# Layers 1 to 3 of a graph network: node phases cut into pieces, messages in steps, TensorE in source order

## The chip, the cores and the metric

The kernel runs on one core of a Trainium2 chip. The metric is the device time of one execution in microseconds (us), median over runs; lower is better. The engines are named as the profile names them: PE is TensorE (PEld its weight loads), DVE is VectorE, ACT is ScalarE, POOL is GpSimd, SP is SyncE, whose queue only issues DMAs.

## The reference

A graph of 12500 nodes with 64 features and 212500 edges (sorted by destination, self-loops among them) goes through four layers; each is wrapped as `x = layernorm(x + layer(x))`:

```
L0  attention, 4 heads:  h = x@W; e = leaky(a_src[src] + a_dst[dst]); softmax over each node's edges; sum of h[src]*alpha
L1  three times:         h = x@Ws[i]; x = relu(segment_sum(norm * h[src], dst) + bs[i]);   then x@W_out + b_out
L2  five times:          h = leaky(x@W1+b1)@W2 + b2;  e = leaky(edge_attr@We1+be1)@We2 + be2
                         x = layernorm(x + segment_sum(h[src]*e*dot_scale, dst)*res_w)*g + b
L3  once:                h = elu((segment_sum(x[src], dst)/count) @ W); batchnorm(h)*gamma + beta
```

Layers 0 and 1 add one more self-loop to every node. There are nine passes over the edges after layer 0: three in layer 1, five in layer 2, one in layer 3.

## The kernel before

The nodes lie in 128 blocks of 98 (`NQ`, `QB`); four blocks are a group (`G`), so 32 groups. A preparation sorts each destination block's edges into 16 columns of 128 slots (`NJ`). Fourteen of them (`NG`) hold rows that a one-hot matmul of the source block makes: `gather_block` (L924) multiplies a source block's table by one-hots `oh` (fp8) for all 128 destination blocks at once, 14 times 3 matmuls of 98x64 (L931), copies the result from PSUM to `hb` on ACT (L932) and writes it to the DRAM table `g_d` (L933, L934). The last two columns are fetched by two indirect gathers on POOL from the plain node table `tq_d` (`fetch`, L1496).

A pass, `run_pass`, walks the 128 destination blocks. `ask(d)` requests a block's data: the destination one-hots `hot` (L1504), in layer 2 the transposed edge attributes `et` (L1808), the rows `hg` from `g_d` (L1494), and the two gathers. It runs `AHEAD` = 4 blocks ahead. In layers 1 and 3 the row itself is the message; in layer 2 `edge_message` makes it: two matmuls of 128x512 (L1783; the profile shows two records for each f32 matmul), bias and leaky relu on ACT and DVE (L1438, L1439), the second dense layer into two PSUM banks (L1792, L1797), a product with `hg` (L1802). `add_up_parts` cuts the f32 message into three bf16 parts that are read in place: `top` is the upper half of each f32, two subtractions (L1520) leave the remainders, and 16 matmuls with `hot` (L1522) sum the 128 slots by destination, all three parts at once. After two blocks `sums` (L1536) adds the three parts from PSUM into `xsum`.

After the fourth block of a group `node(g, ...)` runs the whole node phase: layer 1 `conv_out` (which adds the node's own row `told`) and `conv`, in its third pass `last_conv` (two dense layers, a layernorm and the first layer 2 node network), layer 2 `node2` (layernorm L1414 to L1429, then `node_network`: transposes L1390, L1696, leaky, L1398), layer 3 `node3`. It ends in `spread`: `split3` (L919 to L922) turns the new table into three bf16 parts by turns on ACT and DVE, the table goes to `tq_d`, and four `gather_block` calls follow one another. The one-hots `oh` for them are loaded at the group's start, in `states(g)` (`load_ohs`, L1511).

While layers 0 and 1 run, `pump` issues indirect gathers of edge attributes on POOL (L959), two and one a block by turns in layer 1; `settle` transposes the arrived ones on PE (L948), ACT copies (L950) and writes them to `at_d` for layer 2. A transposition waits for one gathered tile more before it is put into the program.

The order of work: POOL and SP run in the order of the source (`tc.manual_schedule(engines={POOL, SP})`). PE, DVE and ACT are ordered by the framework's scheduler, which places instructions by its own estimate of their times. Every engine executes its list in order. Each PSUM tile is a bank; layer 2 uses all eight (`pgat` 2, `pacc` 1, `pnode` 1, `p1` 2, `pe` 2).

Of the kernel before, what the change touches and what calls it, by code (L numbers as in the profile page):

```python
# [865 lines left out]
def tile_gnn_resnorm_d4(ctx: ExitStack, tc: tile.TileContext, a: dict, out: bass.AP):  # L866
# [70 lines left out]
    room = {}  # L937
# [3 lines left out]
    def settle(keep):  # L941

        while len(late) > keep:
            d, lo, n, ag = late.pop(0)
            pt = room["ps"].tile([P, QA // 4, P], F32, name="pattr", bufs=1)
            for q in range(n // 4):
                tc.keep_in_program_order(
                    pe.transpose(pt[:, q, :], ag[:, 4 * q:4 * q + 4, :].rearrange("p u f -> p (u f)"), ident))  # L948
            ab = room["sb"].tile([P, QA // 4, P], F32, name="ab", bufs=room.get("ab", 1))
            tc.keep_in_program_order(sca.copy(ab[:, :n // 4, :], pt[:, :n // 4, :]))  # L950
# [371 lines left out]
    def network():  # L1322
        with ExitStack() as s0:
# [178 lines left out]
            def load_hot(d):  # L1502
                hot = wk.tile([P, NJ, P], F8, name="hot", bufs=AHEAD + 3)
# [11 lines left out]
            def add_up_parts(hot, x, ps):  # L1515

                top = x.rearrange("p k j f -> p (k j f)").bitcast(BF16).rearrange(
                    "p (k j f h) -> p k j f h", k=3, j=NJ, h=2)[:, :, :, :, 1]
                for k in range(2):
                    v.tensor_tensor(x[:, k + 1], x[:, k], top[:, k], op=OP.subtract)  # L1520
                for j in range(NJ):
# [17 lines left out]
            def run_pass(gd, tab, message, node, states, attrs=(), extra=None):  # L1539
                k = 0  # L1540
                ready = []

                def ask(d):
                    hot = load_hot(d)
                    ex = extra(d) if extra is not None else None
                    ready.append((fetch(d, D, gd, tab, message is None), hot, ex))
# [3 lines left out]
                for g in range(NGR):  # L1550
                    st = states(g)
                    xsum = nt("xsum", DH)[:, :, :D]
                    for pr in range(2):
                        ps = ps_tile([P, 2, 256], "pacc")
                        for i in range(2):
                            d = G * g + 2 * pr + i
                            if d + AHEAD < NQ:
                                ask(d + AHEAD)
                            if attrs:
                                pump(attrs[k % len(attrs)])  # L1560
                                k += 1
                            hg, hot, ex = ready.pop(0)
                            add_up_parts(hot, hg if message is None else message(hg, ex), ps[:, i, :3 * D])
                        sums(xsum, pr, ps, D)
# [374 lines left out]
```

## Time and profile before

| | |
|---|---|
| median of 17 runs | 11363.62 us (11336.18 to 11391.89) |
| the profiled execution | 11402.6 us, span of its instructions 11400.7 us |
| PE busy | 8751.3 us, 77% (weight loads 7324.0 us) |
| DVE busy | 8622.8 us, 76% |
| POOL busy | 6576.8 us, 58% |
| ACT busy | 3871.8 us, 34% |
| DMA | 2414.80 MB, 212 GB/s on average |
| layer 0 begins its gathers | 1652 us |
| first sum of layer 1, of layer 2, of layer 3 | 3539, 5912, 10750 us |

The three passes of layer 1 take 713, 696 and 806 us from their first to their last sum, the five of layer 2 928, 928, 923, 921 and 898 us, that of layer 3 471 us; between one pass's last sum and the next one's first lie 42, 40, 76, 52, 50, 48, 47 and 46 us.

How to read it: shares of the whole span mix stages with different limits, so a table by stage is needed. An engine's busy time leaves out what lies between its instructions: between POOL's gathers the timeline always shows 0.30 us. Ends of matmuls are modelled and overlap with the next one's start; the distance from start to start tells what one costs. A wait that the profile names ("<-") is put down to what ended it.

### The profile page before, as it was taken

To read this page: it belongs to the slowest core of one execution; us is meant where nothing else is said; L and a number is where in the kernel's file an instruction comes from. 1 tells how busy PE (TensorE), PEld (TensorE's weight loads), DVE (VectorE), ACT (ScalarE), POOL (GpSimd) and SP (SyncE) were. 2 spreads that over 40 slices of the span, in tenths; PEclk is the share of its full clock that TensorE was granted. 3 is DMA by queue.
4 is the path that set the end of the run, shared out by engine and by line. 5 is a ranking of instruction groups with operands and counts; after the bars stand their busy time and mean duration, and the time that the engine had idled before them with its cause. 6 is when DMAs were issued, how large, how long until landed. Compare 5 with 4: busy or idle time off the path is not lost.

```text
span 11400.7 us, 260491 instructions
## 1 busy us (share of the span) xinstructions
PE 8751.3 (77%) x102114; PEld 7324.0 (64%) x102115; DVE 8622.8 (76%) x16365; ACT 3871.8 (34%) x7061; POOL 6576.8 (58%) x4616
## 2 busy tenths in 40 slices
PE   2332468888886666667689999999999999899762
PEld 2110458888886665666567777777777777677652
DVE  5889447888885545555568887887887888799888
ACT  2431235455552222222233333333333333333200
POOL 0667578777775767776635544553554555344482
PEclk9855668889987777877789999999999999999875
DMA  2663675555556878877777767776776877677673
GB/s 78 224 224 103 201 244 151 150 153 154 157 151 205 262 249 271 274 246 230 230 238 242 237 212 241 238 239 218 240 241 208 252 241 240 215 250 255 213 212 86
DMA packets 1377992, 2414.80 MB, mean 212 GB/s; under 512 B 421097, under 2 KB 732537, under 8 KB 1376625
## 3 DMA queue, kind: packets, MB, share of 16 engines
q1 hardware_dynamic: 734770, 1565.65, 43.4%
q10 hardware_dynamic: 494495, 714.10, 17.4%
q0 software_dynamic: 147488, 118.29, 6.8%
q8 instruction: 807, 13.22, 0.5%
q14 instruction: 432, 3.54, 0.1%
HBM read 1655.94 MB, written 741.25 MB: 210 GB/s over the span
## 4 chain that ended last, share of the span: by engine, by line
PE 39%; DVE 23%; DMA 19%; issue 8%; ACT 4%; POOL 3%; ACTq 1%; SPq 1%; POOLq 0%; DVEq 0%
PE pacc L1522 8%; PE pe L1797 7%; PE pgat L931 7%; PE p L1783 6%; DMA hg<-tq_d,q_ovr 4%; PE pacc L1532 3%; DMA hg<-g_d 3%; DVE msg L1520 3%; DMA g_d<-hb 3%; PE prank L1603 3%; DVE top L1165 2%; ACT sg L1175 2%; DMA ag<-in_edge_attr_dram,q_eid 2%; PE pnode L1398 2%; DMA slb<-sl_d 2%
## 5 line engine op out<-in xcount | busy, mean ns | idle before, releaser
L1496 POOL DMA_INDIRECT hg<-tq_d,q_ovr x2304 | 3644.4, 1582 | 3130.1 <-DVE msg L1802 1524.7
L959 POOL DMA_INDIRECT ag<-in_edge_attr_dram,q_eid x2048 | 2601.0, 1270 | 1196.5 <-issue 547.0
L931 PE MATMUL pgat<-t,oh 98*128 98x64 bf16 x48384 | 1881.2, 201 | 448.9 <-DVE t L922 195.9
L931 PEld LDWEIGHTS <-oh 98*128 98x128 fp8e4 x48384 | 1801.2, 103 | 643.8 <-issue 620.1
L1522 PEld LDWEIGHTS <-hot 128*128 128x128 fp8e4 x18432 | 1714.1, 103 | 746.1 <-issue 655.3
L932 ACT COPY hb<-pgat 128x448 f32<-128x448 f32 (+1 forms) x2560 | 1302.5, 536 | 2141.7 <-PE pgat L931 1317.8
L1520 DVE TENSOR_TENSOR hg<-hg 128x1024 f32<-128x1024 f32 x1024 | 1237.3, 1220 | 887.2 <-DMA hg<-tq_d,q_ovr 457.0
L1520 DVE TENSOR_TENSOR msg<-msg 128x1024 f32<-128x1024 f32 x1280 | 1557.9, 1217 | 3.9
L1797 PEld LDWEIGHTS pe<-we,eh 128*128 128x128 f32 x10240 | 1364.1, 192 | 225.1 <-issue 140.9
L1797 PE MATMUL pe<-we,eh 128*128 128x128 f32 x10240 | 1469.0, 279 | 4.5 <-DVE eh L1439 3.4
L1438 ACT ACTIVATE eh<-p,be 128x512 f32<-128x512 f32 x1280 | 875.7, 687 | 1567.3 <-PE p L1783 1262.5
L1522 PE MATMUL pacc<-hg,hot 128*128 128x192 bf16 x8192 | 1031.6, 285 | 415.1 <-DVE hg L1520 240.2
L1783 PE MATMUL p<-et,we 128*128 128x512 f32 x2560 | 1290.1, 606 | 22.1 <-DMA et<-at_d 14.7
L1802 DVE TENSOR_TENSOR msg<-pe,hg 128x512 f32<-128x512 f32 x1280 | 862.4, 683 | 322.3 <-PE pe L1797 266.4
L1522 PE MATMUL pacc<-msg,hot 128*128 128x192 bf16 x10240 | 1033.7, 248 | 33.0 <-DVE msg L1520 25.1
L1439 DVE SCALAR_TENSOR_TENSOR eh<-eh 128x512 f32<-128x512 f32 x1280 | 856.9, 682 | 66.2 <-ACT eh L1438 47.1
L1603 PE MATMUL prank<-rv,h 128*128 128x161 f32 x4096 | 742.0, 339 | 202.5 <-DVE rv L1601 162.5
L1603 PEld LDWEIGHTS prank<-rv,h 128*128 128x128 f32 x4096 | 674.7, 218 | 230.7 <-DVE rv L1601 188.1
L1178 PE MATMUL taken<-sg,hotc 128*128 128x456 bf16 x512 | 245.1, 556 | 551.7 <-ACT sg L1175 546.0
L1783 PEld LDWEIGHTS p<-et,we 128*128 128x128 f32 x2560 | 420.6, 192 | 248.1 <-issue 119.4
L1532 PE MATMUL pacc<-msg,o 128*128 128x68 f32 x4096 | 543.3, 295 | 30.7 <-DVE msg L1652 30.7
L1536 DVE TENSOR_REDUCE xsum<-pacc 98x128 f32<-98x384 f32 x576 | 318.0, 552 | 315.2 <-PE pacc L1522 314.1
(327 smaller groups left out, 10278.2 us busy)
## 6 DMA issues: line engine op xcount, KB each, us to landing
hg<-g_d SPq DMA_DIRECT2D x1152, 448.0 KB
g_d<-hb ACTq DMA_DIRECT2D x1152, 416.0 KB
hot<-hot_d SPq DMA_DIRECT2D x1152, 256.0 KB
oh<-oh_d SPq DMA_DIRECT2D x1152, 171.5 KB
et<-at_d SPq DMA_DIRECT2D x640, 256.0 KB
vb<-vw_d SPq DMA_DIRECT2D x128, 912.0 KB
hg<-g_d SPq DMA_DIRECT2D x128, 476.0 KB
g_d<-hb ACTq DMA_DIRECT2D x128, 442.0 KB
```

What stands on the lines that cost most here:

```text
L931: pe.matmul(ps[:, j, :], lhsT=oh[:, 7 * hf + j, :], rhs=t3(k), start=(k == 0), stop=(k == 2))
L932: sca.copy(hb[:, 7 * hf:7 * hf + 7, :], ps)
L959: pool.indirect_dma_start(out=ag[:, j, :], out_offset=None, in_=a["edge_attr_32"], in_offset=bass.IndirectOffsetOnAxis(ap=eid[:, d, lo + j ...
L1438: sca.activation(dst, ps, AF.Identity, bias=bias)
L1496: pool.indirect_dma_start(out=hg[:, NG + i, :], out_offset=None, in_=tab, in_offset=bass.IndirectOffsetOnAxis(ap=ovr[:, d, i:i + 1], axis= ...
L1520: v.tensor_tensor(x[:, k + 1], x[:, k], top[:, k], op=OP.subtract)
L1522: pe.matmul(ps.rearrange("p (k f) -> p k f", k=3), lhsT=hot[:, j, :], rhs=top[:, :, j, :], start=(j == 0), stop=(j == NJ - 1))
L1532: pe.matmul(ps, lhsT=o32[:, j, :], rhs=x[:, hf * nj + j, :], start=(hf + j == 0), stop=(hf == 1 and j == nj - 1))
L1603: pe.matmul(pk[:, i // 2, i % 2, :RANKS * H + 1], lhsT=h32[:, j, :], rhs=rv[:, j, :], start=(hf + j == 0), stop=(hf == 1 and j == nj - 1))
L1783: pe.matmul(p1.rearrange("p q e -> p (q e)"), lhsT=w["we1"][:, j].rearrange("p t d -> p (t d)"), rhs=et, start=True, stop=True)
L1797: pe.matmul(ps[:, u:u + 2, :].rearrange("p t d -> p (t d)"), lhsT=h1[j][:, (2 * hf + q) * P:(2 * hf + q + 1) * P], rhs=w["we2"].rearrange( ...
L1802: v.tensor_tensor(msg[:, half, :], ps, hg[:, half, :], op=OP.mult)
```

## The change

It does five things, all in the part after the preparation.

1. **Node phases in pieces.** The node functions become generators: each `yield` ends a piece. `run_pass` keeps a list `going` and takes one piece of each per block. A transposition, a dense layer, and each of the four `gather_block` calls is a piece of its own: eight pieces for layer 2's node phase, seven in layer 1's first two passes, ten in its third. A group's last gather is so issued up to ten blocks after its last sum. In layer 0 all pieces run at once.
2. **Messages in steps.** Step d does the hidden layer of block d (`first`), message and cut of block d-1 (`second`, `cut`), the sum of block d-2. Without messages (layers 1 and 3) the cut is of block d and the sum of d-1.
3. **PE in the order of the source** in layers 1 to 3 (`tc.manual_schedule(engines={PE})`).
4. **Table parts as upper halves.** `spread` cuts the table as `add_up_parts` cut the messages: two subtractions on DVE in an f32 tile of three parts, the upper halves read in place; no casts on ACT. Layer 0's softmax maxima (`a3`) are cut likewise.
5. **Loads and buffers.** `load_ohs` moves from `states` into `spread`; the buffers of `oh` go from 12 to 8, of `hg` from 6 to 7 (6 in layer 3), of `hot` from 7 to 8.

```
-            def run_pass(gd, tab, message, node, states, attrs=(), extra=None):
...
+            def run_pass(gd, tab, node, states, attrs=(), first=None, second=None, extra=None):
+                lag = 1 if first is None else 2
+                asked, begun, made, going = [], [], [], []
...
+                d = 0
+                while d < NQ + lag or going:
+                    if d + AHEAD < NQ:
+                        ask(d + AHEAD)
+                    if d < NQ:
+                        if attrs:
+                            pump(attrs[k % len(attrs)])
+                            k += 1
+                        full, hot, ex = asked.pop(0)
+                        begun.append((full, hot, None if first is None else first(ex)))
+                    if lag - 1 <= d < NQ + lag - 1:
+                        full, hot, h1 = begun.pop(0)
+                        if first is not None:
+                            full = second(full, h1)
+                        made.append((hot, full, cut(full)))
+                    if lag <= d < NQ + lag:
+                        c = d - lag
+                        g, i = divmod(c, G)
+                        if i == 0:
+                            st = states(g)
+                            xsum = nt("xsum", DH)[:, :, :D]
+                        if i % 2 == 0:
+                            ps = ps_tile([P, 2, 256], "pacc")
+                        hot, full, top = made.pop(0)
+                        add_up_parts(hot, top, ps[:, i % 2, :3 * D])
+                        if i % 2 == 1:
+                            sums(xsum, i // 2, ps, D)
+                    for t in list(going):
+                        if next(t, going) is going:
+                            going.remove(t)
+                    if lag <= d < NQ + lag and i == G - 1:
+                        going.append(node(g, xsum, *st))
+                    d += 1
...
-            def spread(g, t, ohs, cur, also=None):
-                t3 = nw.tile([QB, G, 3, D], BF16, name="t3")
-                split3(nw, t, lambda k: t3[:, :, k, :], [QB, G, D], "ns")
+            def spread(g, t, cur, also=None):
+                ohs = load_ohs(g)
+                top = cut(t)
+                t = t[:, 0]
                 sca.dma_start(group(tq_d[cur], g), t)
                 if also is not None:
                     sca.dma_start(group(also[0], g), also[1])
                 for i in range(G):
-                    gather_block(wk, pp, G * g + i, lambda k, i=i: t3[:, i, k, :], D, g_d[cur], ohs[i], hbbufs)
+                    yield
+                    gather_block(wk, pp, G * g + i, lambda k: top[:, k, i, :], D, g_d[cur], ohs[i], hbbufs)
...
+            def node_network(g, src, w, cur, also=None):
+                yield
+                xt = turned4(src)
+                yield
                 ph = ps_tile([P, G * QB], "pnode")
-                pe.matmul(ph, lhsT=w["w1"], rhs=turned4(src).rearrange("p b n -> p (b n)"), start=True, stop=True)
+                pe.matmul(ph, lhsT=w["w1"], rhs=xt.rearrange("p b n -> p (b n)"), start=True, stop=True)
                 h1 = nw.tile([P, G, QB], F32, name="nh1")
                 leaky(h1.rearrange("p b n -> p (b n)"), ph, w["b1"])
+                yield
                 ps = dense(h1, w["w2"])
...
-            hgbufs, ohbufs, hbbufs = AHEAD + 2, 3 * G, 4
+            hgbufs, ohbufs, hbbufs = AHEAD + 3, 2 * G, 4
             room.update(ag=4, ab=2)
+            phase.enter_context(tc.manual_schedule(engines={PE}))
```

## The prediction, made before the changed kernel was run

> **What bounds the kernel now.** I read the slices first, then one row per pass, then the instructions inside a pass.
>
> From the page:
> ```profile
> span 11400.7 us, 260491 instructions
> ...
> PE   2332468888886666667689999999999999899762
> ...
> DVE  5889447888885545555568887887887888799888
> ...
> POOL 0667578777775767776635544553554555344482
> PEclk9855668889987777877789999999999999999875
> ```
> From about 3500 us to 5900 PE is at 6 and 7, POOL at 7; from there to 10700 PE is at 9, DVE at 7 and 8. Two different limits, so I cut the span at the passes. A pass has 64 sums (L1536), one for two blocks; each row but the first runs from a pass's first sum to its last, that is 126 blocks. The rows: layer 0 whole, the three passes of layer 1, the first and the last pass of layer 2, layer 3. Columns: length, then busy time and count of PE, PEld, DVE, ACT, POOL, then granted clock, DMA share, GB/s.
> ```profile
> 1650.00:3510.00 1860.00, 1552.94 (x16063) 1495.62 (x16064) 1486.17 (x3660) 926.70 (x1375) 1399.35 (x1024) 0.88 0.50 149
> 3539.40:4252.60 713.20, 472.25 (x7436) 440.48 (x7436) 391.08 (x499) 178.72 (x401) 537.11 (x436) 0.80 0.83 261
> 4294.30:4990.30 696.00, 468.64 (x7440) 437.47 (x7440) 391.21 (x499) 178.76 (x405) 534.18 (x431) 0.81 0.86 269
> 5030.30:5835.80 805.50, 571.87 (x7697) 505.64 (x7696) 499.82 (x943) 209.40 (x478) 478.93 (x392) 0.74 0.75 237
> 5911.80:6839.40 927.60, 905.05 (x10248) 717.36 (x10247) 790.30 (x1412) 349.86 (x645) 445.41 (x240) 0.99 0.75 233
> 9807.00:10704.70 897.70, 860.38 (x9940) 681.15 (x9940) 846.12 (x1747) 318.77 (x616) 404.20 (x240) 0.99 0.75 246
> 10750.30:11221.50 471.20, 310.91 (x2388) 273.44 (x2386) 373.63 (x529) 40.62 (x94) 383.18 (x243) 0.77 0.70 203
> ```
> In layer 1 POOL is the limit, though its share does not say so: the timeline shows 0.30 us between any two gathers. Pass 1: 436 gathers of 537.1/436 = 1.23 us plus 0.30 are 5.30 us a block, and a block takes 713.2/126 = 5.66. Pass 2: 5.27 of 5.52. Pass 3: 392 x (1.22 + 0.30) = 4.73 of 6.39; here no engine is full, and 1.66 us a block is waiting. Layer 3: 243 x (1.58 + 0.30) = 3.63 of 3.74. Layer 0: 1024 x (1.37 + 0.30) = 1710 of 1860 us.
>
> In layer 2 the first four passes (927.6, 927.5, 922.6 and 920.8 us) take 7.34 us a block on average. PE's ends are modelled, so I take start to start. PE in the timeline of the fourth of these passes:
> ```profile
> 9306.19 0.22 PE L931 MATMUL pgat<-t,oh 98*128 98x64 bf16 x2 [0.56 <-ACT t L921]
> ...
> 9311.20 1.39 PE L931 MATMUL pgat<-t,oh 98*128 98x64 bf16 x42
> 9312.42 0.25 PE L1522 MATMUL pacc<-msg,hot 128*128 128x192 bf16 x1
> ...
> 9317.36 1.88 PE L1783 MATMUL p<-et,we 128*128 128x512 f32 x4
> 9319.09 1.52 PE L1522 MATMUL pacc<-msg,hot 128*128 128x192 bf16 x16
> 9320.45 1.52 PE L1797 MATMUL pe<-we,eh 128*128 128x128 f32 x12
> 9321.81 1.02 PE L1783 MATMUL p<-et,we 128*128 128x512 f32 x2
> ```
> Undisturbed, a block costs PE 1.73 (four L1783) + 1.36 (sixteen L1522) + 1.81 (sixteen L1797 at 1.36/12) + 0.44 (two L1792 at 0.22) + 1.22 (42 L931), and a group of four blocks 0.85 (L1696) + 0.67 (L1398) + 0.36 (L1390) = 1.88, so 0.47 a block: **7.03 us**. The 0.31 left are stalls like the 0.56 of the first line, where PE stands at a gather until ScalarE has cut a table part (L921). DVE needs 790.3/126 = 6.27. The last pass has no node network: PE 6.56, DVE 846.1/126 = 6.72, measured 7.12.
>
> **The change, part by part.** All terms are against the profiled execution: 11402.6 us, span 11400.7.
>
> *Layer 2, first four passes.* PE now runs in source order, which the order of the built program shows: hidden layer of block d, message of d-1, sum of d-2, then one piece of a node phase, with one block's gather (1.22 us) as the usual piece. No matmul is removed. Each is fed by work of the step before, so the 0.31 mostly goes. I keep 0.05 for DVE, which is 6.27 of 7.08 busy: 7.08 against 7.34 over 504 blocks is **-131 us**. Bounds: at the floor -156; below nothing if DVE's node bursts reach PE (second rival).
>
> *Last pass of layer 2.* DVE is next: 6.72 plus what gaps remain. I take 6.95 against 7.12: **-22** (bounds 0 and -50).
>
> *Table parts.* Before: cast, subtract, cast, subtract (L919 to L922), 0.40 and 0.42 us each, by turns on ACT and DVE. Now two subtracts on DVE; the parts are read in place as upper halves, at every second bf16. That access is not new: L1522 reads its 192 columns so, at 85 ns, and L931's 64 contiguous ones take 29; in proportion to L1522's columns they would take 28, so the stride costs nothing. Gone are two casts a group on ACT, which has time (349.9 of 927.6); they matter only where the chain is bare, between passes.
>
> *Layer 1, passes 1 and 2.* Neither a gather nor a transfer is removed. POOL keeps 5.30 and 5.27, DMA is already at 0.83 and 0.86. I take 5.45 and 5.42: **-26 and -13** (bounds: at POOL's floor -45 and -32; at worst +20 for both, see the clock below).
>
> *Layer 1, pass 3.* Its waits are the node phase's (two transposes, two dense layers, a norm in one chain) and POOL standing behind it. Cut in ten pieces, the chain runs beside the next blocks. What is late next: POOL at 4.73, but a gather that meets DVE work is slower: in the timeline between two layer 2 passes twelve of them take 1.00 us with DVE idle, and the one at 7854.71, beside a pair of L1520, 1.86. The mean is 1.22 here with DVE at 0.62, 1.58 in layer 3 with DVE at 0.79. At 5.6 us a block DVE stands at 3.97/5.6 = 0.71; between the two rows a gather is then about 1.41, and POOL needs 3.11 x 1.71 = 5.3. DMA moves the same bytes: 0.75 x 6.39/5.6 = 0.86, the share of pass 2. I take 5.6: **-100**. Bounds: -145 at 5.25, and -30 if only the lost casts count.
>
> This slowing has a rule. The Trainium skill, "SBUF — State Buffer", section "Who interferes with whom", says that a DVE instruction with two SBUF inputs holds up only a GpSimd instruction that reads SBUF, and infers that generating descriptors is not slowed by it. The rows say otherwise, or an indirect gather counts as a reader: layer 3's 1.58 stands beside two-input subtracts for the most part. By the rule's inference a gather would stay at 1.00 and pass 3 could reach 3.11 x 1.30 = 4.0 on POOL; the sum does not use it.
>
> *The loads of the one-hots* (four of 171.5 KB a group) leave the start of the group and move behind its dense step on SP, past the requests of some eight later blocks. Each request waits for a buffer of three blocks back (seven buffers of `hg` now, six before), so SP still runs two to three steps, 10 us or more, ahead of the gather that needs them. The four issues took 7.93 us at 4513 with SP blocked, 2.78 at 7857 unblocked; I put nothing, and if they come late PE stands for up to 2.8 us a group (bound: 2.8 x 256 = +717, far off, since SP would have to have lost its whole lead).
>
> *In-order waits.* The attribute transposes (L948) can now hold PE when their gather is late. Queued behind is the sum of the block before, and for that POOL's buffers wait. But the gathers of a tile are issued at least 2.7 blocks earlier on POOL, some 14 us, against 4.6 us from the last issue of `g_d` (7844.81) to the load that waits for it (7849.41): nothing, bound +0.3 us for each of layer 1's blocks, +115.
>
> *Between passes* (40 to 76 us, eight times): the chain sum, norm, node network, gathers, write, load stays bare. It loses two casts and their handovers (about 1 us); pieces of the group before now stand in it, with 448 KB of writes each; PE no longer puts the next pass's hidden layer between the last gathers: **-2 each, -16** (+2 to -4 each). *Layer 3*, on POOL: **-3** (bounds -14 and +10). *Layer 0*, on POOL, keeps its scheduled PE: **0** (bounds ±20).
>
> Sum: -131 - 22 - 26 - 13 - 100 - 16 - 3 = **-311**. The profiled execution is 39 us above the median of the 17 runs, 11363.6; off the median, 11363.6 - 311 = 11053, say **11050**.
>
> **The clock.** Layer 1 was granted 0.74 to 0.81, layer 2 0.99 and 1.00; the fourth slice shows 0.5. With PE's work spread thinner the grant may fall. At half, layer 1's blocks would cost PE about twice 2.9 = 5.8 in passes 1 and 2 and twice 3.5 = 7.0 in pass 3 (start to start as above), so PE would bind all three: (0.14 + 0.28 + 0.61) x 126 = +130 in place of -139. Against it: pass 3 of today idles longer at a stretch (its chain) and still gets 0.74.
>
> **Rivals.**
> 1. *Only the chain in layer 1 was bare.* Layer 2's stalls come back as waits for DVE. Then -100 - 39 - 16 - 3 = -158: about 11205. For it: DVE at 0.85. Against: the stalls seen wait on the table parts and node chain.
> 2. *Slower: the norm's burst on DVE.* A layer 2 step gives DVE 2 x 1.22 + 4 x 0.68 + 0.28 = 5.44 us of 7.08, 1.64 to spare; the norm and the line before it add 4.6 us in one or two steps. In source order PE cannot take other work while it stands at a sum. If the overhang of 4.6 - 1.64 = 3 us is not absorbed, each of 160 groups costs PE 3 us: +480 on the -311, about 11530. It starts once DVE trails PE by more than the 3.9 us (hidden layer 1.73, message 1.81 + 0.44) that a step puts ahead of its sum, and ends slower once a group loses more than 311/160 = 1.9 us. The order of the built program spreads the norm over two steps, which speaks against it.
> 3. *Nearly no effect:* layer 1's clock halves (+130) while layer 2 gains (-153), and -19 for the rest: about 11320.
>
> **How the numbers follow.** Forecast 0.63 (10900 to 11140), rival 1 0.20, rival 2 0.12, rival 3 0.05, of which 0.03 within 0.2% (about what a measurement of this kernel can tell from no change) and 0.01 on either side. Faster 0.63 + 0.20 + 0.01 = 0.84, same 0.03, slower 0.12 + 0.01 = 0.13. The range goes from all floors together (-156 - 50 - 77 - 145 - 14 - 32 = -474, about 10900) through rival 1 to 11290, where rival 2 at half its price ends (-311 + 240); 11320 and 11530 stay out.
>
> **What would show it.** Right: four passes near 892 us between first and last sum, PE without waits on table parts, pass 3 near 706, POOL's idle time there gone and its gathers longer. Wrong: PE waiting for `msg` (L1524 then) once a group, PE waiting for the one-hots' DMA or for `ag`, a clock near 0.5 in layer 1, or pass 3 still over 6 us a block.

## The result, and the profile after

The changed kernel takes 11869.5 us (median of 8 runs, 11839.0 to 11889.6) against 11363.6 of the kernel before: a ratio of 1.0441, 95% interval 1.0427 to 1.0454. It is slower, on the other side of the forecast. The profiled execution has a span of 11872.4 us, 472 more than before.

The page's first lines:
```profile
span 11872.4 us, 259968 instructions
...
PE   3331668888876666655579999998998999888762
...
DVE  6889348888765555544458878887887887887788
...
POOL 0666678777657777744434434443443443333382
PEclk9755678888877878766679999999999999888876
```
Two stretches have thinned out: the slices 18 to 20 (5050 to 5940 us), where PE falls to 5 and POOL from 7 to 4, and the slices 35 to 37 (10090 to 10980), where PE is at 8 in place of 9. The passes tell which they are. Rows as for the kernel before: layer 0, the three passes of layer 1, the first and the last pass of layer 2, layer 3 (length, busy time and count of PE, PEld, DVE, ACT, POOL, granted clock, DMA share, GB/s).
```profile
1650.00:3510.00 1860.00, 1576.18 (x16116) 1526.36 (x16117) 1479.29 (x3659) 911.19 (x1252) 1346.31 (x1024) 0.86 0.50 149
3538.70:4224.30 685.60, 456.81 (x7480) 431.42 (x7478) 387.79 (x499) 160.85 (x345) 529.82 (x435) 0.80 0.87 272
4259.60:4941.60 682.00, 452.86 (x7468) 427.71 (x7466) 386.28 (x499) 160.47 (x349) 521.47 (x430) 0.80 0.88 275
4982.20:6051.80 1069.60, 603.30 (x7758) 548.48 (x7756) 508.15 (x951) 196.40 (x423) 465.58 (x390) 0.69 0.58 178
6125.50:7055.80 930.30, 887.64 (x10191) 723.97 (x10190) 803.01 (x1401) 323.46 (x579) 418.28 (x238) 0.99 0.71 230
10088.50:11185.20 1096.70, 905.18 (x9850) 730.87 (x9849) 876.74 (x1744) 299.04 (x552) 381.66 (x238) 0.89 0.62 198
11230.60:11691.80 461.20, 315.43 (x2388) 267.25 (x2386) 373.51 (x528) 40.62 (x94) 373.67 (x243) 0.76 0.70 208
```
Term by term, forecast and measured:

| | forecast us | measured us | off by |
|---|---|---|---|
| layer 1, passes 1 and 2 | -26, -13 | -27, -14 | -2 |
| layer 1, pass 3 | -100 | +264 | +364 |
| layer 2, first four passes (930.3, 930.1, 930.4, 930.3) | -131 | +22 | +153 |
| layer 2, last pass | -22 | +199 | +221 |
| the eight gaps between passes | -16 | +37 | +53 |
| layer 3 | -3 | -10 | -7 |

The six terms add up to 471 of the 472 us; layer 0 (forecast 0) ended 0.7 us earlier. No engine has much more to do: in the third pass of layer 1 DVE's busy time rose by 8 us and PE's by 31, while its granted clock fell from 0.74 to 0.69; the pass rose by 264. The loss is standing. This is who stands, in each place.

**Layer 2, first four passes.** PE, between two sums of one of them:
```profile
7617.47 1.52 PE L1530 MATMUL pacc<-msg,hot 128*128 128x192 bf16 x16
7618.83 1.40 PE L931 MATMUL pgat<-tnew,oh 98*128 98x64 bf16 x42
7621.40 0.53 PE L1390 MATMUL pnode<-q_ident,x 98*64 98x98 f32 x4 [1.16 <-DVE x L1429]
```
PE stands once a group at the transposes, until DVE's last line of the norm (L1429): 170.8 us in the four passes together. The stalls at the table parts (L921 before) are gone, but they were small: in the kernel before, all of PE's waits in its four passes sum to 63.0 us, 10.2 of them at table parts.

**Layer 2, last pass.** PE, then DVE, around one group's first gather:
```profile
10715.83 1.52 PE L1530 MATMUL pacc<-msg,hot 128*128 128x192 bf16 x16
10723.02 0.21 PE L931 MATMUL pgat<-tnew,oh 98*128 98x64 bf16 x1 [5.67 <-DMA hot<-hot_d]
...
10725.95 2.61 PE L1825 MATMUL p<-et,we 128*128 128x512 f32 x4
```
```profile
10722.45 0.42 DVE L1425 TENSOR_TENSOR tnew<-y,ln_r 98x256 f32<-98x256 f32 x1
10722.91 0.89 DVE L1524 TENSOR_TENSOR tnew<-tnew 98x256 f32<-98x256 f32 x2
10729.71 0.69 DVE L1849 TENSOR_TENSOR msg<-pe,hg 128x512 f32<-128x512 f32 x1 [5.91 <-PE pe L1844]
```
The name behind PE's 5.67 is a load of `hot`, which this matmul does not read; what it reads and waits for is `tnew`, whose norm ends at 10722.87. (Of PE's 191.5 us of waits in this pass 81.0 are put down to that line of the norm, 96.5 to `hot`.) Only then can PE go on to the next hidden layer, and now DVE stands 5.91 us for the message. The two engines, each about 7 us busy a block by the row (905.2 and 876.7 over 126), take turns, and a block takes 8.7.

**Layer 1, pass 3.** PE, DVE and POOL in the same 20 us:
```profile
5501.01 1.61 PE L931 MATMUL pgat<-tnew,oh 98*128 98x64 bf16 x42
5514.31 0.86 PE L1390 MATMUL pnode<-q_ident,x 98*64 98x98 f32 x4 [11.69 <-DVE x L1425]
```
```profile
5504.93 0.41 DVE L1420 TENSOR_REDUCE ln_var<-ln_sq 98x4 f32<-98x256 f32 x1
5510.42 1.23 DVE L1524 TENSOR_TENSOR hg<-hg 128x1024 f32<-128x1024 f32 x1 [5.08 <-issue]
...
5513.83 0.43 DVE L1425 TENSOR_TENSOR x<-y,ln_r 98x256 f32<-98x256 f32 x1
```
```profile
5502.79 1.75 POOL L1496 DMA_INDIRECT hg<-tq_d,q_ovr  x1 [0.31 <-issue]
...
5518.00 0.99 POOL L1496 DMA_INDIRECT hg<-tq_d,q_ovr  x1 [10.81 <-PE pacc L1530]
```
PE waits for the norm's end. DVE is in the middle of the norm and stands before a cut. That cut needs rows whose second gather POOL began at 5502.79, since only PE's last sum, ending at 5501.2, had freed the buffer; the gather's packets ended at 5510.2 in the trace, and the cut began. POOL's next gather waits for PE's next sum. It is a ring of PE, POOL and DVE that turns once a group. DVE's instructions are placed by the scheduler, which puts the cuts as far ahead of the sums as the seven buffers allow.

I give the ring a number, the *room*: the sums ahead of a group's transposes on PE, plus the buffers, less the blocks cut ahead of the norm's last line on DVE. At 0, the last cut ahead of the norm waits for the very sum behind which PE stands. Sums and cuts are counted in blocks from the pass's start, by the order in the trace. The third group has 16 sums, 7 buffers, 23 cuts: 16 + 7 - 23 = 0, and 28 of the 32 groups have 0. The kernel before had 5 to 6.

**Gaps in layer 2.** PE, then SP's queue, at the start of the third pass:
```profile
8068.81 2.40 PE L931 MATMUL pgat<-tnew,oh 98*128 98x64 bf16 x42 [0.46 <-ACT hb L932]
8082.47 3.40 PE L1825 MATMUL p<-et,we 128*128 128x512 f32 x4 [11.26 <-DMA et<-at_d]
```
```profile
8058.33 0.60 SPq L1484 DMA_DIRECT2D we<-in_L_gnn_We_dram  x1
8075.31 0.35 SPq L1494 DMA_DIRECT2D hg<-g_d  x1
...
8076.19 0.42 SPq L1855 DMA_DIRECT2D et<-at_d  x1
```
Before, the hidden layer of the next pass ran between the last gathers. Now its attributes `et` are asked for behind the first `hg` load, since the new `ask` calls `fetch` first, and that load waits for the pass before to write `g_d`: SP issues nothing from 8058.93 to 8075.31.

### The profile page after: what moved, and what is told of

It is laid out like the page before. It is cut to its first block, busy times and chain, and to the rows that moved or that the text cites. A ratio compares the mean times of both kernels' runs of the same rounds, so it can differ in the third digit from the quotient of the medians.

```text
span 11872.4 us, 259968 instructions
## 1 busy us (share of the span) xinstructions
PE 8790.6 (74%) x102114; PEld 7482.1 (63%) x102115; DVE 8716.5 (73%) x16365; ACT 3673.4 (31%) x6423; POOL 6354.5 (54%) x4616
## 4 chain that ended last, share of the span: by engine, by line
PE 42%; DVE 28%; DMA 14%; issue 8%; ACT 3%; POOL 2%; SPq 1%; ACTq 0%; POOLq 0%; DVEq 0%
PE pgat L931 8%; PE p L1825 8%; PE pacc L1530 8%; PE pe L1844 7%; DVE msg L1524 4%; PE pacc L1540 4%; DMA hg<-tq_d,q_ovr 4%; PE prank L1636 3%; DVE msg L1849 3%; DVE hg L1524 2%; DVE top L1165 2%; DVE eh L1439 2%; DMA slb<-sl_d 2%; ACT sg L1175 2%; DMA hg<-g_d 2%
## 5 line engine op out<-in xcount | busy, mean ns | idle before, releaser
L1496 POOL DMA_INDIRECT hg<-tq_d,q_ovr x2304 | 3465.8, 1504 | 3971.0 <-DVE msg L1849 2183.3
L959 POOL DMA_INDIRECT ag<-in_edge_attr_dram,q_eid x2048 | 2562.7, 1251 | 984.4 <-issue 578.4
L932 ACT COPY hb<-pgat 128x448 f32<-128x448 f32 (+1 forms) x2560 | 1350.6, 535 | 3877.8 <-PE pgat L931 2835.4
L931 PE MATMUL pgat<-tnew,oh 98*128 98x64 bf16 x48384 | 1861.2, 200 | 724.1 <-DVE tnew L1719 321.5
L1524 DVE TENSOR_TENSOR hg<-hg 128x1024 f32<-128x1024 f32 x1024 | 1242.8, 1220 | 1146.8 <-DMA hg<-tq_d,q_ovr 592.8
L1530 PEld LDWEIGHTS <-hot 128*128 128x128 fp8e4 x18432 | 1767.1, 104 | 255.9 <-issue 163.6
L1524 DVE TENSOR_TENSOR msg<-msg 128x1024 f32<-128x1024 f32 x1280 | 1561.0, 1220 | 13.7
L1844 PE MATMUL pe<-we,eh 128*128 128x128 f32 x10240 | 1355.9, 276 | 0.0
L1530 PE MATMUL pacc<-msg,hot 128*128 128x192 bf16 x10240 | 977.7, 247 | 1.5 <-DVE msg L1524 0.9
L1825 PEld LDWEIGHTS p<-et,we 128*128 128x128 f32 x2560 | 456.5, 199 | 470.2 <-issue 336.1
L1540 PE MATMUL pacc<-msg,o 128*128 128x68 f32 x4096 | 581.8, 310 | 79.1 <-DVE msg L1684 77.6
L1540 PEld LDWEIGHTS pacc<-msg,o 128*128 128x128 f32 x4096 | 566.1, 224 | 92.3 <-DVE msg L1684 68.4
```

Of the source, the lines that this page charges most:

```text
L931: pe.matmul(ps[:, j, :], lhsT=oh[:, 7 * hf + j, :], rhs=t3(k), start=(k == 0), stop=(k == 2))
L932: sca.copy(hb[:, 7 * hf:7 * hf + 7, :], ps)
L959: pool.indirect_dma_start(out=ag[:, j, :], out_offset=None, in_=a["edge_attr_32"], in_offset=bass.IndirectOffsetOnAxis(ap=eid[:, d, lo + j ...
L1496: pool.indirect_dma_start(out=hg[:, NG + i, :], out_offset=None, in_=tab, in_offset=bass.IndirectOffsetOnAxis(ap=ovr[:, d, i:i + 1], axis= ...
L1530: pe.matmul(ps.rearrange("p (k f) -> p k f", k=3), lhsT=hot[:, j, :], rhs=top[:, :, j, :], start=(j == 0), stop=(j == NJ - 1))
L1540: pe.matmul(ps, lhsT=o32[:, j, :], rhs=x[:, hf * nj + j, :], start=(hf + j == 0), stop=(hf == 1 and j == nj - 1))
```

## The experiments

Theory 1: the norm stands too near, in the source, to the piece of PE that needs it. Theory 2: in layer 1's third pass the scheduled cuts close the ring. Theory 3: the order of the first loads makes the gaps. The main rival is that DVE or POOL is simply full, or that the table parts or the pieces cost something.

The runs came in five sets, each beside runs of the kernel before on the same chip. Two of the sets ran on chips where the kernel before takes 12442 and 12472 us, not about 11350; there layer 0, the first two passes of layer 1 and the gaps are longer in every kernel, layer 2's passes are the same, and the third pass of layer 1 is longer in some kernels and not in others. So those two sets are compared within themselves. Edits without an interval have one run each.

### One cause at a time

*An extra step behind the norm.*
```diff
 def node_network(g, src, w, cur, also=None):
     yield
+    yield
...
                         layernorm(y2, full[:, 0])
+                        yield
```


> One edit on the changed kernel: a node phase does nothing for one more step behind a layer norm (at the head of the node network, and behind the second norm of layer 2's last pass), so that DVE has a whole step more before TensorE reaches the piece that needs the norm. Theory 1 (TensorE in source order stands at the piece behind the norm, since the norm takes DVE more than one step): layer 2's first four passes go from 930 us each to 880 to 895 (the 0.34 us a block at the transposes goes), the last pass from 1097 to 870 to 920, layer 1's third pass from 1070 to 850 or less. Theory 2 (in layer 1's third pass DVE's own order, with cuts 5 to 7 blocks ahead of the sums, closes a loop through the buffers of gathered rows): layer 2 as in theory 1, but the third pass of layer 1 stays over 950, since the norm still stands behind a cut whose rows wait for TensorE. Rival (DVE is simply full, the standing is where its lack of time shows): all passes within 10 us of the changed kernel.

Measured: 11438.9 us. Rows of layer 1's third pass, then the first and the last of layer 2:
```profile
4970.10:6028.40 1058.30, 574.18 (x7715) 524.88 (x7713) 499.47 (x949) 185.00 (x421) 440.54 (x390) 0.71 0.58 179
6101.90:6980.30 878.40, 875.75 (x10148) 717.85 (x10147) 799.30 (x1401) 317.09 (x576) 369.61 (x238) 1.00 0.77 243
9872.20:10751.10 878.90, 833.68 (x9800) 686.22 (x9798) 852.43 (x1739) 294.77 (x550) 420.80 (x238) 0.99 0.77 246
```
Layer 2 is as theory 1 says: 930 to 878 and 1097 to 879, by one `yield` each. DVE does the same work in it, so it was not full. Layer 1's third pass stays at 1058, as theory 2 says: room there is still 0 (17 sums, 24 cuts).

*VectorE in source order in layer 1.*
```diff
-            phase.enter_context(tc.manual_schedule(engines={PE}))
+            phase.enter_context(tc.manual_schedule(engines={PE, DVE}))
```


> One edit on the changed kernel: in layer 1 VectorE's instructions too stand in the order of the source (there a cut stands one block ahead of its sum, not 5 to 7). Nothing changes in layers 2 and 3. Theory 2 (loop through VectorE's look-ahead): the third pass of layer 1 goes from 1070 us to 690 to 780, passes 1 and 2 stay within 15 us of 686 and 682. Theory 1 alone (the norm is too near to the transposes, wherever the cuts stand): the third pass keeps over 950 us. Rival (POOL: gathers slowed by VectorE's work bind the third pass): it stays over 1000 us, with no waits of TensorE on L1425 but on the cuts.

Measured: 11440.5 us. Layer 1's first and third pass:
```profile
3549.00:4193.50 644.50, 452.38 (x7482) 428.40 (x7481) 409.19 (x501) 156.04 (x345) 506.11 (x435) 0.82 0.92 290
4907.10:5633.30 726.20, 546.82 (x7801) 489.58 (x7800) 543.27 (x962) 195.52 (x426) 447.32 (x390) 0.81 0.84 264
```
Theory 2 holds: 1070 to 726, with room 7 (12 sums, 12 cuts). Passes 1 and 2 fell too, to 644 and 642, which no theory had said (expected: within 15 of 686 and 682).

*Each block's small loads first*, one-hots and attributes ahead of gathered rows, as before the change:
```diff
-                    asked.append((fetch(d, D, gd, tab, first is None), load_hot(d),
-                                  extra(d) if extra is not None else None))
+                    hot = load_hot(d)
+                    ex = extra(d) if extra is not None else None
+                    asked.append((fetch(d, D, gd, tab, first is None), hot, ex))
```


> One edit on the changed kernel: a block's one-hots and edge attributes are asked for ahead of its gathered rows, as in the kernel before. Theory 3 (at the start of a layer 2 pass the attributes stand on SP behind a load of gathered rows, which waits for the pass before to write them, so the hidden layers of the first blocks cannot run in the gap): the four gaps between layer 2's passes go from 60.3, 59.2, 62.5, 59.9 us to 46 to 54 each, together 30 to 55 us less; the passes themselves stay within 10 us. Rival (the gaps are longer because the pieces of the last groups and the one-hots' loads stand in the chain): gaps within 3 us of the changed kernel's.

Measured: 11854.2 us; the four gaps 54.3, 53.4, 56.6 and 54.0, 23.6 us less together. Half of theory 3's effect (expected 30 to 55, and no gap over 54): now the second block's attributes stood behind the first block's rows, 10.8 us.

*PE placed by the scheduler again*, all else as changed (the three `manual_schedule` lines taken out):

> One edit on the changed kernel: TensorE's instructions are placed by the scheduler in layers 1 to 3 again, and all else (pieces, steps, cuts, order of loads) stays. If the order of the source is what costs: layer 2's last pass falls from 1097 us to 850 to 900, layer 1's third pass from 1070 to 690 to 810, layer 2's first four from 930 to 890 to 925. If the pieces or the two subtracts that take the place of two casts on ScalarE cost it (VectorE's work, more of it and on one engine): the last pass of layer 2 stays over 1050 us and the third of layer 1 over 1000.

Measured: 11207.3 us, against 11343.8 of the kernel before on the same chip (one run each). Third pass of layer 1, first and last of layer 2:
```profile
4990.10:5743.60 753.50, 569.74 (x7509) 493.25 (x7506) 498.85 (x928) 176.95 (x409) 473.13 (x389) 0.76 0.79 247
5831.50:6724.90 893.40, 885.80 (x10191) 717.57 (x10191) 793.12 (x1400) 315.29 (x579) 405.55 (x238) 1.00 0.75 240
9647.80:10515.10 867.30, 832.19 (x9786) 677.81 (x9798) 834.87 (x1739) 292.87 (x550) 469.27 (x238) 1.00 0.75 249
```
So the rest of the change is a gain (-31 us a pass in layer 2's first four against the mean 924.7 of before), and PE's order of the source alone turned it into a loss. The gaps in layer 2 stay at 59.4 to 61.3 us: they do not come from PE's order.

### On a chip with longer layers 0 and 1 (kernel before: 12442 us)

*The first two edits, and the first loads ahead.* The last is this:
```diff
-                for d in range(AHEAD):
-                    ask(d)
+                for d, soon in enumerate([early(d) for d in range(AHEAD)]):
+                    ask(d, soon)
```
where `early(d)` loads a block's one-hots and attributes, and `ask` then only fetches.

> Three edits on the changed kernel: the extra step behind a norm, VectorE in source order in layer 1, and, at the start of every pass, the one-hots and edge attributes of the first blocks asked for ahead of all gathered rows. If the three causes are separate, their measured gains add: layer 2 as with the extra step alone (878 us a pass), layer 1 as with VectorE in order (644, 642, 726 or less), the four gaps between layer 2's passes 46 to 54 us instead of 60: a span of 10950 to 11010, 3 to 4% under the kernel before. If they share a cause, the span stays over 11100.

Measured: ratio 0.968 (0.965 to 0.971). Layer 2 at 878.5, 878.8, 878.9, 878.8 and 876.8; layer 1's passes take 739, 731 and 971 us and layer 2's gaps 66.1 to 68.1, which say nothing beside the set before.

*VectorE in source order in layers 2 and 3* (the same edit of `engines` there):

> One edit on the changed kernel: in layers 2 and 3 VectorE's instructions too stand in the order of the source (no extra step; layer 1 as in the changed kernel). It asks whether in layer 2 the norm is too near by the source alone, or by where the scheduler puts its second half on VectorE. By nearness alone: layer 2's passes keep 915 to 940 us and the last one over 1000. By VectorE's scheduled order: 880 to 905 and 870 to 930. Layer 3 has no norm in its pass and cuts 1 to 3 blocks ahead: 461 us within 10.

Measured: 911.4, 909.7, 911.6, 910.1 and 1062.7; layer 3 463.2. The last pass lies inside the band for nearness, and PE still stands 100 us there for `tnew`: the norm is too near by the source. The first four lie just under the band, but not for that reason. PE and DVE there:
```profile
9848.54 0.53 PE L1390 MATMUL pnode<-q_ident,x 98*64 98x98 f32 x4
...
9853.92 1.53 PE L1530 MATMUL pacc<-msg,hot 128*128 128x192 bf16 x16 [0.90 <-DVE xsum L1544]
```
```profile
9848.05 0.43 DVE L1429 TENSOR_TENSOR x<-y,b 98x256 f32<-98x256 f32 x1
...
9853.32 0.55 DVE L1544 TENSOR_REDUCE xsum<-pacc 98x128 f32<-98x384 f32 x1
```
With the norm in one piece PE's standing at the transposes falls from 170.8 to 15.0 us in the four passes. DVE is late by the norm instead, and PE stands 89.9 us at a sum, until `xsum` has emptied the one bank `pacc`. So there the late norm comes from where the scheduler puts its second half; without that the burst costs PE at the sum, some 20 us a pass less.

*Table parts as upper halves alone, on the kernel before*, in layers 1 to 3 (`top` is the view of the upper halves of `t`, which now has three planes):
```diff
-                t3 = nw.tile([QB, G, 3, D], BF16, name="t3")
-                split3(nw, t, lambda k: t3[:, :, k, :], [QB, G, D], "ns")
+                for k in range(2):
+                    v.tensor_tensor(t[:, k + 1], t[:, k], top[:, k], op=OP.subtract)
```


> One part of the change alone, on the kernel before: in layers 1 to 3 the table parts are upper halves (two subtracts on VectorE, read by TensorE at every second bf16) and no longer two casts and two subtracts by turns. If that access cost TensorE anything, layer 2's first four passes would grow by its share (42 matmuls a block: 10% on each is 0.12 us a block, 15 us a pass). If it costs nothing, they stay within 5 us or fall by up to 20 (the stalls at the gathers), the gaps fall by 1 to 2 us each, and the whole is 0 to 0.7% faster than before. In either case the loss of the whole change, 4.4%, is not here.

Measured: ratio 1.0049 (1.0032 to 1.0067), a little slower, not faster as expected; run again below.

*First loads ahead alone:*

> One edit on the changed kernel: at the start of every pass the one-hots and attributes of all the first blocks are asked for ahead of any gathered rows (with only each block's own order turned round, the second block's attributes still stood behind the first block's rows, 10.8 us, and the gaps fell by 6 us each). Theory 3: the four gaps between layer 2's passes go to 45 to 51 us from 60. Rival (the rest is the writes and the one-hots' loads of the last groups): they stay at 53 or more. The passes stay within 10 us.

Measured: 64.5, 63.7, 65.1 and 59.4 us, which this chip leaves open (the run with VectorE in order in layers 2 and 3, whose loads are the changed kernel's, had 72.9 to 73.8).

### The same again where the kernel before takes 11350 us, and two steps in place of one

> The kernel with the three edits once more (extra step, VectorE in order in layer 1, first loads ahead): the set before ran on a chip where the kernel before took 12442 us and layers 0 and 1 were longer for every kernel, so its layer 1 and its gaps say nothing beside the first set. Where the kernel before takes about 11350: separate causes give layer 1 passes of 640 to 650, 640 to 650 and 690 to 730, layer 2 passes of 878, gaps between them of 46 to 55 and a whole of 10930 to 11010, a ratio of 0.965 to 0.972. If the extra step and VectorE's order are one cause in layer 1, the third pass stays at 726 or more.

Measured: 11033.7 us, ratio 0.9719 (0.9703 to 0.9736); gaps 52.2 to 53.6; passes of layer 1 650, 641 and **782**: worse than with VectorE in order alone (726).

> First loads ahead alone, once more beside a kernel before of about 11350 us. Theory 3 alone: the four gaps between layer 2's passes 45 to 51 us (60 in the changed kernel, 54 with only each block's order turned round). Rival (the rest is writes and one-hot loads of the last groups): 53 or more.

Measured: gaps of 50.3, 49.7, 48.5 and 44.4 us, those of the kernel before (52.5 to 46.5). Theory 3 holds. PE at the start of the same pass now goes from the last gather to the hidden layers at once:
```profile
8080.02 1.40 PE L931 MATMUL pgat<-tnew,oh 98*128 98x64 bf16 x42 [0.47 <-ACT hb L932]
8081.25 3.87 PE L1828 MATMUL p<-et,we 128*128 128x512 f32 x8
```

> Table parts as upper halves alone, on the kernel before, once more: on the other chip it was 0.5% slower (interval 0.3 to 0.7%), against the expectation of 0 to 0.7% faster. If the parts themselves cost, the ratio is 1.003 to 1.007 here too and the loss stands in layer 2's last pass (922 us there; 898 in the kernel before) and in the other passes of layer 2 by 4 to 8 us. If that was the chip's slow layers 0 and 1, layer 2 is within 5 us a pass and the ratio 0.993 to 1.000.

Measured: ratio 1.0010 (0.9999 to 1.0021). First pass of layer 1, first and last of layer 2:
```profile
3512.10:4202.30 690.20, 469.48 (x7523) 438.45 (x7523) 392.12 (x501) 156.00 (x345) 528.59 (x435) 0.78 0.87 272
5835.50:6762.60 927.10, 906.32 (x10367) 720.56 (x10410) 793.21 (x1411) 332.36 (x591) 421.77 (x241) 1.00 0.73 235
9731.60:10653.00 921.40, 858.96 (x9812) 683.78 (x9823) 841.89 (x1747) 294.79 (x550) 430.62 (x240) 0.99 0.73 239
```
Reading every second bf16 costs PE next to nothing: from start to start a matmul of a gather takes 29.6 ns against 29.2, and the four passes 927.0 us on average against 924.7. The parts alone give 34 of the 41 us that passes 1 and 2 of layer 1 gained (690 and 685, against 713 and 696), and take back 24 us in layer 2's last pass, twice (921.4, 922.3 on the other chip). There PE's waits rose from 32.5 to 58.0 us, those at a gather for ACT's copy `hb` from 7.3 to 28.5. Why the copies come late stays open; with the pieces that loss is not seen (867 to 879).

*Two extra steps* (one more `yield` at both places):

> Two extra steps behind a norm instead of one, on the changed kernel: a dose for theory 1. If one step is all that the norm needed, layer 2's passes stay at 878 us within 3 (TensorE has no standing left to lose) and only the gaps grow, by 3 to 7 us each as they did with the first step (60 to 65). If a part of the standing were left with one step, the passes fall by another 5 us or more.

Measured: 11121.5 us. Layer 2 at 876.3, 876.3, 876.3, 876.1 and 877.8: one step was enough. The gaps grew by only 1.4 us on average (expected 3 to 7). But layer 1's third pass fell from 1058 to 746, with its cuts still some 5 blocks ahead of the sums:
```profile
4966.40:5712.90 746.50, 528.12 (x7671) 486.43 (x7670) 489.55 (x947) 185.38 (x419) 475.62 (x389) 0.80 0.81 253
```
So it isn't look-ahead by itself that costs: room is now 2 (26 sums, 31 cuts), and the ring is open.

### Room, and why two cures were worse than one

*VectorE in order in layer 1, the extra step in layer 2 alone, first loads ahead* (kernel before: 12472 us for this set):

> VectorE in source order in layer 1, the extra step behind a norm in layer 2 alone, first loads ahead. Beside the kernel with the three edits (11034 us, third pass of layer 1 at 782 us): if the extra step is what costs there once VectorE is in order, the third pass is back at 720 to 735 and the whole at 10960 to 11000 (0.966 to 0.969 of the kernel before). If the order of the first loads (one-hots ahead of gathered rows) costs it, it stays at 770 to 790 and the whole at 11030.

Measured: ratio 0.9642 (0.9626 to 0.9658); passes of layer 1 740, 743 and 885 us, the third outside both bands, on this chip.

*Two, and three, extra steps in layer 1's third pass alone*, the first with one buffer less:
```diff
                 layernorm(y2, x2)
+                yield
+                yield
                 yield from node_network(g, x2, w, 1 - cur, (x_d, x2))
...
-            hgbufs, ohbufs, hbbufs = AHEAD + 3, 2 * G, 4
+            hgbufs, ohbufs, hbbufs = AHEAD + 2, 2 * G, 4
```


> On the changed kernel: two extra steps behind the norm in layer 1's third pass alone, and six buffers of gathered rows in layer 1, not seven. By the built order the room (sums ahead of the transposes, plus buffers, less blocks cut ahead of the norm) is 2 blocks, as with two steps and seven buffers. Room's theory: the third pass takes 740 to 770 us. If it is the number of buffers that counts: over 850. Layer 2 as in the changed kernel (930, 1097); passes 1 and 2 of layer 1 within 20 us of 686 and 682.

> On the changed kernel: three extra steps behind the norm in layer 1's third pass alone, seven buffers. By the built order the room is 4 blocks. Room's theory: 710 to 750 us, no slower than with room 2 (746). If each step has a price of its own inside the pass (as both edits together seemed to say): over 760. All else as in the changed kernel.

Measured: 748.7 us with six buffers and room 2, 767.9 with seven and room 4, both far from the 1072 and 1066 of room 0 on such chips. So the number of buffers isn't what counts; opening the ring is. Above 2 the room brought nothing more (expected 710 to 750; by the trace it settles at 3.5). Over 760 was expected if each step has a price, but passes 1 and 2, without extra steps, are 21 and 13 us longer in that run too, so the 19 us say little.

*Passes apart:* VectorE in order in passes 1 and 2, two steps in pass 3, the step in layer 2, first loads ahead:

> VectorE in source order in passes 1 and 2 of layer 1 alone; the third pass has a scheduled VectorE and two extra steps behind its norm (room 2); the extra step in layer 2; first loads ahead. The third pass takes 740 to 760 us on either kind of chip. Where the kernel before takes 11350: 644 and 642 for passes 1 and 2, 878 for layer 2's, a whole of 10980 to 11020. Where it takes 12450: passes 1 and 2 at 735 to 745, a whole of 11850 to 11920.

> VectorE in source order in all three passes of layer 1, the extra step in layer 2 alone, first loads ahead, once more. Where the kernel before takes 11350: third pass 720 to 735 if the extra step in layer 1 made 782 out of 726, 770 to 790 if the order of the first loads did; whole 10960 to 11000 or 11030. Where it takes 12450: 885 again, and the whole 100 to 150 us over the kernel with the passes apart.

Measured side by side: 10993.1 us, ratio 0.9687 (0.9660 to 0.9713), and 11001.3, 0.9688 (0.9663 to 0.9712). Both beat both kernels. With the passes apart, first and third pass of layer 1, first and last of layer 2:
```profile
3538.20:4175.60 637.40, 448.65 (x7481) 424.44 (x7481) 409.34 (x501) 155.91 (x345) 499.30 (x434) 0.82 0.92 293
4892.00:5628.90 736.90, 530.67 (x7674) 489.07 (x7673) 490.37 (x946) 185.45 (x419) 495.57 (x392) 0.80 0.82 256
5703.20:6581.60 878.40, 875.80 (x10146) 718.00 (x10145) 798.86 (x1400) 315.51 (x576) 368.76 (x238) 1.00 0.78 244
9429.20:10307.00 877.80, 833.64 (x9801) 685.71 (x9799) 852.19 (x1738) 294.34 (x550) 420.58 (x238) 0.99 0.81 250
```
In the other kernel the third pass is back at 735. It differs from the one that took 782 only by the extra step in layer 1, so that step costs some 47 us once VectorE is in order (86 on the other kind of chip, 971 against 885); the order of loads is cleared. The trace suggests how (VectorE in order stands longer for ScalarE's `nh` and `ln_s`: 1.6 us a block against 1.1), but no run isolates that.

All third passes, by the kind of chip:

| kernel | room | third pass us, kernel before at about 11350 | at about 12450 |
|---|---|---|---|
| before (with the table parts alone) | 5 to 6 | 805 (798) | (970) |
| changed, or with edits elsewhere | 0 | 1070, 1073, 1067 | 1066, 1072 |
| one step | 0 | 1058 | |
| two steps | 2 | 746, 737 | |
| two steps, six buffers | 2 | | 749 |
| three steps | 4 | | 768 |
| PE scheduled | 6 | 754 | |
| VectorE in order | 7 | 726, 735 | 885 |
| VectorE in order, one step | 8 | 782 | 971 |

Room 0 goes with about 1070 us on either kind of chip, and every edit that opens the ring is far below on the first kind. From 2 up the time does not follow the room: on the second kind VectorE in order, with room 7, takes 136 us more than two steps with room 2. What costs there is open.

## Why the prediction was wrong, step by step

- **Layer 2, first four passes.** The failed step: "Each is fed by work of the step before, so the 0.31 mostly goes. I keep 0.05 for DVE". PE's own 7.03 was right (a block takes 6.97 with the extra step). But a norm of 4.6 us does not fit into the 1.64 us that a step leaves on DVE; it ends in the step after, where PE already stands. (The 5.44 behind the 1.64 adds durations, which overlap on DVE. With VectorE in order a step's share takes 5.2 us from start to start, which leaves 1.9; the norm does not fit into that either.) Measured is 0.34 us of PE's standing a block. The 0.31 was misread too: PE's waits before were 63.0 us over 504 blocks, 0.12 a block, and 0.02 of it at table parts. Most of the rest was busy time: the first pass has PE 905 us busy before and 876 with the extra step, with only 1% fewer matmuls in the stretch. Why, no run shows. I had counted "the order of the built program spreads the norm over two steps" against the second rival; it is just what makes the norm late here: with the norm in one piece the standing at the transposes falls to 15.0 us in four passes.
- **Layer 2, last pass.** "DVE is next" was true, but not the bound. PE stands 1.52 us a block, 6.1 a group, for the second norm and the cut behind it, and the block forecast as 0.17 better is 1.58 worse. With the extra step it takes 6.98, near the forecast 6.95.
- **The second rival** named the right burst, but the place and the price were off. It had PE standing at a sum, for `msg`, at 3 us a group; PE stands at the piece that needs the norm. In layer 2's first four passes that was 0.34 x 4 = 1.4 us a group, half the price; the last pass lost 199/32 = 6.2 a group, since DVE stands in turn. Layer 1's third pass, where the most was lost (264/32 = 8.3 a group), it did not mention, nor did any other rival. So 11870 lies beyond its 11530.
- **Layer 1, pass 3.** The failed step: "Cut in ten pieces, the chain runs beside the next blocks. What is late next: POOL at 4.73". Next was the norm, behind a cut that waits for PE: PE stood there, and the pass took 8.49 us a block in place of 5.6. With the ring opened by two steps it takes 5.92. I costed POOL and the clock and never laid DVE's built order beside PE's, which shows room 0 before any run.
- **Between passes.** I named what PE gives up ("PE no longer puts the next pass's hidden layer between the last gathers") and bounded it at +2 a gap. In layer 2 it was +7.8 to +14.5. I had followed the one-hots of the node phase past SP's queue, but not the new order of `fetch` and the attributes inside `ask`.
- **Layer 1, passes 1 and 2.** Size right, reason wrong, so the hit is luck: I had put the lost casts down as worthless outside the gaps, and the table parts alone give 34 of the 41 us. Nor is 5.30 us a block a floor: with VectorE in order a block takes 644.5/126 = 5.11.
- **Right:** the table parts' stride is nearly free (29.2 and 29.5 ns a matmul); the moved one-hots make PE wait 0.3 us in all of layer 1's passes; layer 3 and layer 0; the clock (third rival) did not halve, 0.69 to 0.80 in layer 1. The in-order attribute transposes, put at nothing, hold PE for 33 us in the three passes of layer 1, inside the bound of 115; with VectorE in order they hold it for 109 and 105 us in passes 1 and 2, which still gain.

## What to carry to other kernels

Where one engine runs in source order and another in a scheduler's, lay the two orders side by side and count: work that the first engine must finish, plus buffers, less what the second has put ahead of its answer. At zero the engines stand in turn, though none is full. One step more between question and answer cured layer 2; in the ring of layer 1 it left the room at zero and cured nothing, and two steps opened it, so count again after each edit. A room above zero says that the ring is open, not which kernel is fastest. And when a time lands in the expected band, look whether the wait is the expected one. When loads are regrouped in a helper, read which of them now stand behind one that waits.

## What the hardware showed beyond that

The indirect gathers' length goes with what VectorE does beside them, not only with how much: with the same cuts in another order the 435 gathers of layer 1's first pass took 506.1 us in place of 529.8 (1.16 us each against 1.22), the shortest still 1.00. The prediction had weighed this against the Trainium skill, "SBUF — State Buffer", section "Who interferes with whom", which infers that a two-input instruction of VectorE does not slow the generating of descriptors. After the change the gathers beside the two-input cut (L1524) average 1.34 us in layer 1's first pass and 1.80 in layer 2's, and 1.00 where VectorE is idle. So either the inference does not hold for indirect gathers, or they count as instructions that read SBUF, which the same section says such a cut holds up; no run separates the two.

On the chips with longer layers 0 and 1, PE stands for microseconds in the middle of a gather's matmuls with no wait to show (first loads ahead, on the first of those chips, in a gap):
```profile
8842.81 0.85 PE L931 MATMUL pgat<-tnew,oh 98*128 98x64 bf16 x13 [5.95 <-issue]
```
What holds it there was not tried.
